# A graph network's two expert layers: branch arms for eight widths, and row fetches queued earlier

## The chip, the core and the metric

The kernel runs on one core of a Trainium2 chip, in one launch. The metric is device time in microseconds (us). The engines are TensorE (PE, matmuls), VectorE (DVE), ScalarE (ACT), GpSimd (POOL, which also issues indirect DMAs) and SyncE (SP, which issues DMAs). Each has its own instruction stream; "PEldq" in the profile is the sequencer that feeds PE with instructions.

## What is computed

Two layers over 1250 nodes of 1024 features, all in float32. Each layer adds a graph convolution and an attention mix to x, and then a mixture of experts (cut; names shortened):

```python
x = x + gcn(xn, edges) + mix0(xn)
x = x + experts0(layernorm(x))
x = x + sage(xn, edges) + mix1(xn)
x = x + experts1(layernorm(x))

# experts0: 8 experts, each takes its best at most 391 tokens
top_g, tok_idx = top_k(gates.T, cap)
xe = x[tok_idx]
h = silu(xe @ gate_w[e]) * (xe @ up_w[e])          # 1024 -> 512
out[tok_idx] += (h @ down_w[e]) * top_g            # 512 -> 1024

# experts1: 8 experts, every token goes to its best 2, no cap
hidden = silu(h1) * h2                             # 1024 -> 256 each
y = sum(prob * (hidden @ w3[e]))                   # 256 -> 1024
```

How many tokens an expert gets depends on the data. For these inputs the first layer's experts get 318, 358, 263, 231, 330, 366, 391 (its cap) and 237. In the second layer an expert's tokens are cut into units of at most 512; of 12 possible units ten are used, with 276, 384, 131, 394, 1, 384, 173, 17, 384 and 356 tokens.

## The kernel before

Tokens lie along a matmul's columns: for a block of 128 hidden features, a weight tile of 128x128 is loaded and the tokens of the expert (n columns) are streamed past it, over eight blocks k of the 1024 input features. Since n is known only at run time, `by_width` (L192) writes each piece of work once per possible width, as arms of a binary tree of `tc.If`, and every engine that has work in it branches to the arm whose width is the smallest that holds the count.

**First experts (L859 to L900).** For each of 8 experts, and each of four blocks i of hidden features, one piece computes gate and up (L868: 8 logical matmuls each), then the SiLU on ACT (L870) and the product on DVE (L871). It has four arms, 248, 296, 344 and 392 columns. Down is two pieces of four output blocks of four logical matmuls each (L888), with a transpose of each bank by DVE. The rows of the next expert are fetched by POOL (`rows_for`) and transposed by DVE (`columns`); its weights, 2 MB each for gate, up and down, are loaded by SP as their buffers come free.

**Second experts (L1358 to L1424).** `units_from(u, ...)` writes unit u and calls itself for the next. A unit loads the weights of unit u+1, computes gate and up for two blocks of hidden features (L1383; a piece is both, in four arms of 128, 256, 384 and 512 columns), lets DVE transpose the rows of unit u+1 (`turn`, L1372, with arms of its own), and computes down (L1401) per block of 128 tokens, where the tokens are the stationary operand and 512 output features are the columns. Each block's result goes through `ye` (six buffers; DVE L1406 and ACT L1404) and is added to the output by an indirect DMA of POOL (L1407, the scatter). `fetch(u)` (L1345) issues on POOL the indirect DMAs that bring the rows of unit u, 32 at a time by quarters (12 for 384 tokens), into `xq1`, which has two buffers. From unit 5 on a unit lies in a `tc.If` of its own (`when`, L1329).

The order of instructions on each engine is that of the program, as far as a scheduler doesn't move independent ones; POOL works through fetches and scatters strictly in that order, and so does DVE through h3T (L1387), the turn and ye. `tc.keep_in_program_order` pins the weight loads.

Of the kernel before, what the change touches and what calls it, by code (L numbers as in the profile page):

```python
# [10 lines left out]
F32 = mybir.dt.float32  # L11
# [11 lines left out]
P = 128  # L23
N = 1250
D = 1024
KB = D // P
# [13 lines left out]
H1 = 256  # L40
CAP = 391
SLOTS = 392
WIDTHS = [248, 296, 344, SLOTS]
B = 32
NI = 13
NG = 4
# [3 lines left out]
UC = 4  # L50
NU = 12
COLS = NU * UC
COUNTS = [P * (c + 1) for c in range(UC)]
LN_EPS = 1e-5
EXACT = 4096.0

# [47 lines left out]
def network(tc: tile.TileContext, a: dict, out: bass.AP, env: SimpleNamespace, exact: bool):  # L104
    nc = tc.nc
# [6 lines left out]
    turn = [0]  # L112
# [8 lines left out]
    def bank(name):  # L121
        return psum.tile([P, 512], F32, name=name, tag="bank")
# [69 lines left out]
    def by_width(n, widths, work):  # L192

        if len(widths) == 1:
            return work(widths[0])
        m = len(widths) // 2
        with tc.If(n <= widths[m - 1]) as cmp:  # L197
            by_width(n, widths[:m], work)
        with cmp.Else():
            by_width(n, widths[m:], work)  # L200
# [602 lines left out]
    with s_route:  # L803
        quarters = x1n_d.rearrange("n (j f) -> (n j) f", j=4)
        with tc.tile_pool(name="moe0", bufs=1) as mp:
            def first_columns():

                xeT = mp.tile([P, KB, ROWS], F32, name="xeT", bufs=2)
                room = [mp.tile([P, NI, B, KB], F32, name=n).rearrange("p i c b -> p (i c b)") for n in ("xq", "ye")]
                for g in range(NG):  # L810
                    n = min(P, SLOTS - g * P)
                    xe = room[g // 3][:, g % 3 * D:(g % 3 + 1) * D]
                    nc.gpsimd.indirect_dma_start(
                        out=xe, out_offset=None, in_=x1n_d,
                        in_offset=bass.IndirectOffsetOnAxis(ap=idx[:, g:g + 1], axis=0))
                    for b0 in (0, 4):
                        pt = bank("pte")
                        for b in range(4):
                            nc.tensor.transpose(pt[:, b * P:b * P + n], xe[:n, b0 + b::KB], ident[:n, :n])
                        evac(xeT[:, b0:b0 + 4, g * P:g * P + n], pt.rearrange("p (b q) -> p b q", b=4)[:, :, :n])  # L820
                return xeT

            def rows_for(e):
                xq = mp.tile([P, NI, B, KB], F32, name="xq")
                for i in range(NI):
                    g = e * NG + i // 4
                    nc.gpsimd.indirect_dma_start(
                        out=xq[:, i].rearrange("p c b -> p (c b)"), out_offset=None, in_=quarters,
                        in_offset=bass.IndirectOffsetOnAxis(ap=idx_q[:, i % 4, g:g + 1], axis=0))
                return xq  # L830

            def columns(xq):
                xeT = mp.tile([P, KB, ROWS], F32, name="xeT", bufs=2)
                for i0 in range(0, NI, 4):
                    i1 = min(i0 + 4, NI)
                    nc.vector.transpose(xeT.rearrange("p b (i r) -> p i b r", r=B)[:, i0:i1],
                                        xq[:, i0:i1].rearrange("p i c b -> p i b c"))
                return xeT

            def weights(e):  # L840
                wg, wu = (wpool.tile([P, KB, I0], F32, name=n, tag="w") for n in ("wg", "wu"))
                for w, name in ((wg, "gate"), (wu, "up")):
                    nc.sync.dma_start(w, a[f"L0_ffn_{name}_w"][e].rearrange("(p k) f -> p k f", k=KB))
                wd = mp.tile([P, I0 // P, D], F32, name="wd")

                load = (nc.sync if e else nc.scalar).dma_start(wd, a["L0_ffn_down_w"][e].rearrange("(k p) f -> p k f", p=P))
                if e == 0:
                    tc.keep_in_program_order(load)
                return wg, wu, wd

            xeT = first_columns()
            ws = weights(0)

            number = [nc.values_load(taken[0:1, e:e + 1], min_val=0, max_val=CAP) for e in range(E)]
            for e in range(E):
                wg, wu, wd = ws
                hT = mp.tile([P, I0 // P, SLOTS], F32, name="hT")
                if e + 1 < E:
                    xq = rows_for(e + 1)  # L859
                for i in range(I0 // P):  # L860
                    ic = slice(i * P, (i + 1) * P)
                    pg, pu = bank("pgate"), bank("pup")
                    sg = mp.tile([P, SLOTS], F32, name="sg", bufs=2)

                    def gate_up(n):
                        for pw, w in ((pg, wg), (pu, wu)):
                            for k in range(KB):
                                nc.tensor.matmul(pw[:, :n], w[:, k, ic], xeT[:, k, :n],  # L868
                                                 start=(k == 0), stop=(k == KB - 1))
                        nc.scalar.activation(sg[:, :n], pg[:, :n], AF.Silu)  # L870
                        nc.vector.tensor_mul(hT[:, i, :n], sg[:, :n], pu[:, :n])  # L871

                    by_width(number[e], WIDTHS, gate_up)
                    if i == 1:

                        wdb = mp.tile([P, I0 // P, KB, P], F32, name="wdb")
                        for j in range(I0 // P):
                            nc.scalar.copy(wdb[:, j], wd[:, j].rearrange("p (q b) -> p b q", b=KB))  # L878
                if e + 1 < E:
                    xeT = columns(xq)  # L880
                ye = mp.tile([P, NI, B, KB], F32, name="ye")
                for b0 in range(0, KB, 4):
                    pys = [bank("py") for _ in range(4)]

                    def down(n):
                        for b, py in enumerate(pys, b0):
                            for i in range(I0 // P):
                                nc.tensor.matmul(py[:, :n], wdb[:, i, b, :], hT[:, i, :n],  # L888
                                                 start=(i == 0), stop=(i == I0 // P - 1))
                            nc.vector.memset(py[:, n:ROWS], 0.0)  # L890
                            nc.vector.transpose(ye[:, :, :, b], py[:, :ROWS].rearrange("p (i r) -> p i r", r=B))

                    by_width(number[e], WIDTHS, down)
                for j in range(4):
                    (nc.sync if e == E - 1 and j % 2 else nc.scalar).dma_start(
                        env.y_d[e * ROWS:(e + 1) * ROWS, j * KB * B:(j + 1) * KB * B].rearrange("(i r) f -> r i f", r=B),
                        ye[j * B:(j + 1) * B].rearrange("p i c b -> p i (c b)"))
                if e + 1 < E:
                    ws = weights(e + 1)
# [400 lines left out]
    with tc.tile_pool(name="moe1", bufs=2) as ep:  # L1300
# [28 lines left out]
        def when(u, work):  # L1329

            if u < 5:
                return work()
            with tc.If(number[u] >= 1):
                work()
# [22 lines left out]

        def units_from(u, xeT, ws, coming):  # L1358
            later = u + 1 < NU
            if u + 2 < NU:  # L1360
                coming.append(fetch(u + 2))
            if later:
                xq = coming.pop(0)
                xeT2 = ep.tile([P, KB, UC * P], F32, name="xeT1")
# [7 lines left out]
                    nc.vector.transpose(xeT2.rearrange("p b (i r) -> p i b r", r=B)[:, i0:i1],  # L1372
                                        xq[:, i0:i1].rearrange("p i c b -> p i b c"))

            def unit():
                if later:
                    when(u + 1, lambda: load_unit(ws2, which[u + 1], queues[u + 1][0]))
                for i in range(H1 // P):
                    def gate_up(n):
                        p1, p2 = bank("p1"), bank("p2")  # L1380
                        for pw_, off in ((p1, 0), (p2, H1)):
                            for k in range(KB):
                                nc.tensor.matmul(pw_[:, :n], w12[:, k, off + i * P:off + (i + 1) * P], xeT[:, k, :n],  # L1383
                                                 start=(k == 0), stop=(k == KB - 1))
                        sg = ep.tile([P, UC * P], F32, name="sg1")
                        nc.scalar.activation(sg[:, :n], p1[:, :n], AF.Silu)
                        nc.vector.tensor_mul(hT[:, i, :n], sg[:, :n], p2[:, :n])  # L1387

                    by_width(number[u], COUNTS, gate_up)
                if later:  # L1390
                    when(u + 1, lambda: by_width(number[u + 1], COUNTS, turn))

                def down(n):
                    sent = []
                    for c in range(n // P):
# [21 lines left out]
                if later and u == NU - 2:  # L1417
                    units_from(u + 1, xeT2, ws2, coming)

            when(u, unit)  # L1420
            if later and not (u == NU - 2):
                units_from(u + 1, xeT2, ws2, coming)

        units_from(0, xeT, ws, [fetch(1)])  # L1424
    s_moe.close()


# [47 lines left out]
```

## Time and profile before

| | |
|---|---|
| median of 3 runs | 3427.32 us (3417.03 to 3428.79) |
| the profiled execution | 3425.42 us |
| its span, first to last instruction | 3423.7 us |
| mean granted TensorE clock | 0.968 |
| first experts' matmuls | 1215.8 to about 1655 us |
| second experts' matmuls | 3118.1 to 3402.9 us |
| bytes moved by DMA | 317.59 MB, 93 GB/s on average |

In a group's row, "x512" is the number of instructions, the three numbers are the shortest, median and longest in ns, and the shapes follow with their counts. A row of waits reads "engine, what waited <- what it waited for: total us, times, longest". A row of the timeline gives start, duration, engine, line and operation, and in brackets the idle time before it and what ended that. A wait "<- issue" is one for which the trace shows no semaphore: the engine's own sequencer had not delivered the instruction. Matmul durations overlap, since they are pipelined; the time from one start to the next is what one costs.

### The profile page before, as it was taken

Reading aid. Unit: us, or ns where it says so; the run is one execution under the profiler, and the core shown is the slowest. Engines: PE = TensorE matmul, PEld = TensorE weight load, DVE = VectorE, ACT = ScalarE, POOL = GpSimd, SP = SyncE. Lnnn points to the kernel's source line nnn. Section 1 sums busy time; section 2 is a strip of 40 time slices with the busy share of each in tenths; the row PEclk is TensorE's granted clock in tenths of the full one; section 3 lists DMA queues with packets and bytes.
Section 4 is the critical chain, followed back from the end, with each engine's and each line's share of the span. In section 5 each row is a group of like instructions: output and inputs, shape, how many; then the busy total and the mean of one; then the engine's idle time right before and its main releaser. Section 6 shows DMA issues by size and latency. Waiting matters only on the chain. (4 is left out here: it accounts for less than half of the span.)

```text
span 3423.7 us, 30825 instructions
## 1 busy us (share of the span) xinstructions
PE 3254.8 (95%) x11704; PEld 1966.0 (57%) x11704; DVE 941.5 (27%) x2398; ACT 359.2 (10%) x623; POOL 635.7 (19%) x543
## 2 busy tenths in 40 slices
PE   6999999999999789999699999999999999996987
PEld 3474656554557556766445555447777555564553
DVE  4148335531113632322440000011111111234221
ACT  1001011100004211111111011000000000001100
POOL 0006787032001041210100000110000000004432
PEclk9999999999998689999899999999999999997998
DMA  4715222054114054653640000220000110126662
GB/s 155 161 62 138 25 1 26 25 161 143 64 45 144 32 202 149 207 193 111 187 150 25 25 25 25 74 99 28 25 25 25 37 59 32 72 92 235 180 194 53
DMA packets 147591, 317.59 MB, mean 93 GB/s; under 512 B 38951, under 2 KB 60366, under 8 KB 143884
## 3 DMA queue, kind: packets, MB, share of 16 engines
q1 hardware_dynamic: 82108, 216.85, 18.6%
q0 software_dynamic: 40240, 48.25, 7.1%
q10 hardware_dynamic: 24992, 49.16, 4.7%
q8 instruction: 156, 2.56, 0.3%
q14 instruction: 95, 0.78, 0.1%
HBM read 239.25 MB, written 77.82 MB: 93 GB/s over the span
## 5 line engine op out<-in xcount | busy, mean ns | idle before, releaser
L276 POOL DMA_INDIRECT adj_d<-cnt,cell x167 | 261.4, 1565 | 89.3 <-issue 40.6
L1383 PE MATMUL p<-xeT,w 128*128 128x384 f32 (+3 forms) x640 | 179.0, 442 | 9.8 <-DVE ye L1406 5.9
L189 POOL TENSOR_TENSOR xr<-xr,bo 128x512 f32<-128x512 f32 (+1 forms) x40 | 50.4, 1265 | 712.4 <-DMA xr<-res_d 543.2
L1383 PEld LDWEIGHTS p<-xeT,w 128*128 128x128 f32 x640 | 114.0, 194 | 77.0 <-issue 27.0
L165 PE MATMUL pqk<-wk,x0T 128*128 128x512 f32 (+1 forms) x320 | 145.4, 609 | 8.9 <-ACT x0T L117 7.5
L868 PE MATMUL pgate<-xeT,wg 128*128 128x392 f32 (+3 forms) x512 | 151.0, 449 | 2.3 <-DVE py L890 2.0
L888 PE MATMUL py<-hT,wdb 128*128 128x392 f32 (+3 forms) x512 | 145.8, 444 | 4.1 <-ACT wdb L878 4.0
L868 PE MATMUL pup<-xeT,wu 128*128 128x392 f32 (+3 forms) x512 | 148.2, 443 | 0.0
L165 PE MATMUL pv<-wv,x1T 128*128 128x512 f32 (+1 forms) x320 | 141.9, 601 | 4.5 <-ACT x1T L117 2.5
L165 PE MATMUL ph<-ws,h1T 128*128 128x512 f32 (+1 forms) x320 | 143.2, 596 | 0.0
L165 PE MATMUL pqk<-wq,x0T 128*128 128x512 f32 (+1 forms) x320 | 140.7, 593 | 0.0
L165 PE MATMUL ppn<-wn,x1T 128*128 128x256 f32 (+1 forms) x640 | 138.8, 379 | 0.0
L1064 PE MATMUL ph<-x1T,ws 128*128 128x416 f32 (+1 forms) x384 | 138.2, 512 | 0.0
L165 PE MATMUL pv<-wv,x0T 128*128 128x512 f32 (+1 forms) x320 | 138.0, 592 | 0.0
L165 PE MATMUL ph<-wgcn,x0T 128*128 128x512 f32 (+1 forms) x320 | 138.0, 593 | 0.0
L165 PE MATMUL pwo<-wo,attn0T 128*128 128x512 f32 (+1 forms) x320 | 137.7, 593 | 0.2 <-ACT attn0T L433 0.2
L165 PE MATMUL ppn<-wn,h1T 128*128 128x512 f32 (+1 forms) x320 | 137.7, 592 | 0.0
L165 PE MATMUL pwo<-wo,attn1T 128*128 128x512 f32 (+1 forms) x320 | 137.5, 592 | 0.0
L940 PE MATMUL pqT<-x1T,wk 128*128 128x416 f32 (+1 forms) x384 | 135.6, 512 | 0.0
L940 PE MATMUL pqT<-x1T,wq 128*128 128x416 f32 (+1 forms) x384 | 135.6, 512 | 0.0
L165 PEld LDWEIGHTS ppn<-wn,x1T 128*128 128x128 f32 (+1 forms) x640 | 120.0, 188 | 17.7
L868 PEld LDWEIGHTS pgate<-xeT,wg 128*128 128x128 f32 x512 | 98.7, 193 | 49.4 <-issue 4.8
(383 smaller groups left out, 4469.3 us busy)
## 6 DMA issues: line engine op xcount, KB each, us to landing
wg<-in_L_ffn_gate_w_dram SPq DMA_DIRECT2D x8, 2048.0 KB
wu<-in_L_ffn_up_w_dram SPq DMA_DIRECT2D x8, 2048.0 KB
w<-in_L_ffn_w_dram SPq DMA_DIRECT2D x8, 2048.0 KB
wd<-in_L_ffn_down_w_dram SPq DMA_DIRECT2D x7, 2048.0 KB
y_d<-ye ACTq DMA_DIRECT2D x30, 416.0 KB
adj_d<-ezero SPq DMA_DIRECT2D x2, 6105.0 KB
res_d<-xr SPq DMA_DIRECT2D x45, 256.0 KB
table<-adj_d ACTq DMA_DIRECT2D x36, 312.5 KB
```

The lines of the kernel that those rows point to most:

```text
L165: nc.tensor.matmul(pr[:TS[t], :cols], xT[:, k, TOK[t]], w[:, k, :], start=(k == 0), stop=(k == nk - 1))
L189: nc.gpsimd.tensor_add(xr[:TS[t]], xr[:TS[t]], bias[:TS[t]])
L276: nc.gpsimd.indirect_dma_start(out=adj_d[e % 2], out_offset=bass.IndirectOffsetOnAxis(ap=cell[:, e:e + 1], axis=0), in_=cnt[:, e:e + 1], i ...
L868: nc.tensor.matmul(pw[:, :n], w[:, k, ic], xeT[:, k, :n], start=(k == 0), stop=(k == KB - 1))
L888: nc.tensor.matmul(py[:, :n], wdb[:, i, b, :], hT[:, i, :n], start=(i == 0), stop=(i == I0 // P - 1))
L940: nc.tensor.matmul(pq[:, :n], w[:, k, pair * P:(pair + 1) * P], xT[:, k, c0:c0 + n], start=(k == 0), stop=(k == KB - 1))
L1064: nc.tensor.matmul(ps[:, :n], w[:, k, q0 + f * P:q0 + (f + 1) * P], xT[:, k, c0:c0 + n], start=(k == 0), stop=(k == KB - 1))
L1383: nc.tensor.matmul(pw_[:, :n], w12[:, k, off + i * P:off + (i + 1) * P], xeT[:, k, :n], start=(k == 0), stop=(k == KB - 1))
```

## The change

First experts: the widths become eight, 224 to 392 in steps of 24. Gate and up become pieces of their own, and down becomes four pieces of two output blocks instead of two of four. Second experts: gate and up get eight widths from 64 to 512 in steps of 64 and are pieces of their own; where a width is not a whole block of 128, DVE zeroes the rest of the block in h3T, since down keeps whole blocks. The fetch for a unit is written two calls ahead instead of one: `fetch(u + 3)` stands between the turn of unit u+1 and the down of unit u, ahead of that unit's scatters, and `unit` is cut in two for it.

```diff
-WIDTHS = [248, 296, 344, SLOTS]
+WIDTHS = [224, 248, 272, 296, 320, 344, 368, 392]
...
+WIDTHS1 = [64, 128, 192, 256, 320, 384, 448, 512]
...
-                    def gate_up(n):
-                        for pw, w in ((pg, wg), (pu, wu)):
-                            for k in range(KB):
-                                nc.tensor.matmul(pw[:, :n], w[:, k, ic], xeT[:, k, :n],
-                                                 start=(k == 0), stop=(k == KB - 1))
+                    def product(p, w, n):
+                        for k in range(KB):
+                            nc.tensor.matmul(p[:, :n], w[:, k, ic], xeT[:, k, :n], start=(k == 0), stop=(k == KB - 1))
+
+                    def gate(n):
+                        product(pg, wg, n)
                         nc.scalar.activation(sg[:, :n], pg[:, :n], AF.Silu)
+
+                    def up(n):
+                        product(pu, wu, n)
                         nc.vector.tensor_mul(hT[:, i, :n], sg[:, :n], pu[:, :n])
 
-                    by_width(number[e], WIDTHS, gate_up)
+                    by_width(number[e], WIDTHS, gate)
+                    by_width(number[e], WIDTHS, up)
...
-                for b0 in range(0, KB, 4):
-                    pys = [bank("py") for _ in range(4)]
+                for b0 in range(0, KB, 2):
+                    pys = [bank("py") for _ in range(2)]
...
-            if u + 2 < NU:
-                coming.append(fetch(u + 2))
...
-            def unit():
+            def up_to_down():
                 if later:
                     when(u + 1, lambda: load_unit(ws2, which[u + 1], queues[u + 1][0]))
                 for i in range(H1 // P):
...
+                    def gate1(n):
+                        product(p1, 0, n)
                         nc.scalar.activation(sg[:, :n], p1[:, :n], AF.Silu)
+
+                    def up1(n):
+                        product(p2, H1, n)
+                        m = -(-n // P) * P
                         nc.vector.tensor_mul(hT[:, i, :n], sg[:, :n], p2[:, :n])
-
-                    by_width(number[u], COUNTS, gate_up)
-                if later:
-                    when(u + 1, lambda: by_width(number[u + 1], COUNTS, turn))
-
+                        if n < m:
+                            nc.vector.memset(hT[:, i, n:m], 0.0)
+
+                    by_width(number[u], WIDTHS1, gate1)
+                    by_width(number[u], WIDTHS1, up1)
+
+            when(u, up_to_down)
+            if later:
+                when(u + 1, lambda: by_width(number[u + 1], COUNTS, turn))
+
+            if u + 3 < NU:
+                coming.append(fetch(u + 3))
+
+            def from_down():
                 def down(n):
...
-            when(u, unit)
+            when(u, from_down)
...
-        units_from(0, xeT, ws, [fetch(1)])
+        units_from(0, xeT, ws, [fetch(1), fetch(2)])
```

More of the change, by code (lines that the diff above doesn't have):

```diff
@@ L1378, in unit, with product @@
                 for i in range(H1 // P):
[L1379 to L1385, printed above, removed]
+                    p1, p2 = bank("p1"), bank("p2")
+                    sg = ep.tile([P, UC * P], F32, name="sg1")
+                    def product(p, off, n):
+                        for k in range(KB):
+                            nc.tensor.matmul(p[:, :n], w12[:, k, off + i * P:off + (i + 1) * P], xeT[:, k, :n],
+                                             start=(k == 0), stop=(k == KB - 1))
+                    def gate1(n):
+                        product(p1, 0, n)
                         nc.scalar.activation(sg[:, :n], p1[:, :n], AF.Silu)
+                    def up1(n):
+                        product(p2, H1, n)
+                        m = -(-n // P) * P
                         nc.vector.tensor_mul(hT[:, i, :n], sg[:, :n], p2[:, :n])
-                    by_width(number[u], COUNTS, gate_up)
-                if later:
-                    when(u + 1, lambda: by_width(number[u + 1], COUNTS, turn))
+                        if n < m:
[8 more added lines that the diff above has]
+            def from_down():
                 def down(n):
```

## The prediction

> **What bounds the kernel now.** I read the page's first two parts, then the groups by line, then the waits of TensorE (PE) in the two stages that the diff touches, then the branch records of its sequencer and the timeline where it stood still.
>
> ```profile
> PE 3254.8 (95%) x11704; PEld 1966.0 (57%) x11704; DVE 941.5 (27%) x2398; ACT 359.2 (10%) x623; POOL 635.7 (19%) x543
> ...
> q8 instruction: 156, 2.56, 0.3%
> ```
>
> PE is busy 95% of 3423.7 us, so matmul time that is taken away is time gained, unless PE then waits for something. Queue 8 brings code: 156 fetches of 2.56 MB in all, 16,384 bytes each. It looks harmless as a share; I come back to it.
>
> ```profile
> L868 PE MATMUL pgate<-xeT,wg x512: 372/453/913, 1215.8 to 1636.4; 128*128 128x392 f32 x64, 128*128 128x344 f32 x43, 128*128 128x248 f32 x43, 128*128 128x296 f32 x21
> L1383 PE MATMUL p<-xeT,w x640: 273/486/1008, 3118.1 to 3392.0; 128*128 128x384 f32 x80, 128*128 128x256 f32 x32, 128*128 128x128 f32 x32, 128*128 128x512 f32 x16
> ```
>
> These durations are of overlapping, pipelined matmuls. From start to start one takes 209 ns at 248 columns, 249 at 296, 289 at 344, 329 at 392, 323 at 384 and 429 at 512: 0.84 ns per column. Each logical f32 matmul is two recorded ones: 192 per first expert (64 gate, 64 up, 64 down), 64 gate and up per second unit and 8 per block of 128 rows in its down. In the first stage PE waits only 6 us in all. In the second (3118 to 3424):
>
> ```profile
> PE py L1401 <- DVE h3T L1387: 6.3, 1, 6.3
> PE p L1383 <- DVE ye L1406: 5.9, 2, 5.3
> PE p L1383 <- issue: 3.9, 1, 3.9
> PE py L1401 <- issue: 0.8, 1, 0.8
> ```
>
> The first is unit 7 at 3328.7: DVE stood 5.40 us in the turn (L1372) for unit 8's rows, and this unit's h3T was queued behind it. The second is unit 0 at 3149.4: DVE stood 5.88 us for unit 1's rows, with ye (L1406) behind it. The "issue" ones are PE's own sequencer:
>
> ```profile
> L197 PEldq COMPARE_BRANCH  x265: 64/179/5449, 1215.3 to 3395.0; - x133
> ```
>
> ```profile
> 3251.52 7.31 PE L1383 MATMUL p<-xeT,w 128*128 128x128 f32 x64
> ...
> 3258.66 3.60 PE L1401 MATMUL py<-w,h3T 128*128 128x512 f32 x8
> ...
> 3266.12 1.62 PE L1383 MATMUL p<-xeT,w 128*128 128x384 f32 x2 [3.86 <-issue]
> ```
>
> A branch usually takes 64 to 450 ns, but some took 3.92, 4.80, 5.14 and 5.45 us. The last began at 3260.38, after unit 4, whose matmuls are only 128 wide: PE ran dry for 3.86 us. Beside the fetch records the reason shows. Code comes one block ahead: the fetch of the next block starts when the sequencer enters a block, and a branch into it ends about 1.4 us after its transfer of 1.0 us is over. From entering to start is 1.05 us in most of the first stage, but 3.6 to 3.9 us while the next expert's weights load (1320 to 1330: DMA share 1.0, 400 GB/s), and in the second stage between 3180 and 3335 a median of 4.1 us. A block per 3.5 us is thus the pace in quiet stretches, 6.2 to 6.5 us in busy ones. What covers it is the lead: the sequencer runs 18 recorded matmuls ahead of the array, 5.2 us at 344 columns, 7.7 us behind 512-wide downs, 2.0 us at 128.
>
> **The change, part by part.** The sum is against the profiled execution's 3425.4 us; the median of the runs shown is 3427.3, 1.9 us above it.
>
> *Widths in the first experts.* The counts in the inputs are 318, 358, 263, 231, 330, 366, 391 and 237; the widths go from 344, 392, 296, 248, 344, 392, 392, 248 to 320, 368, 272, 248, 344, 368, 392, 248. Four experts lose 24 columns: 4 x 192 x 24 x 0.84 ns = **-15.5 us**, all on PE's path, since PE hardly waits there.
>
> *Widths in the second units.* Counts 276, 384, 131, 394, 1, 384, 173, 17, 384, 356. Gate and up lose 64 columns in units 0, 2, 3 and 6: 64 x 64 x 0.84 ns = 3.4 us each. Unit 0's is lost again: its end waits for rows whose fetch PE doesn't release, and that wait grows by what PE saves. So **-10.3 us**. Units 4 and 7 go from 128 to 64 columns; what says what that is worth? A 128-wide f32 matmul here starts each 112 ns, and so do the 65-wide ones at L368 and even 8-wide ones: no gain. [...] The row decides: 0. Down keeps whole blocks of 128.
>
> *Row fetches ahead of scatters.* In the built order only two things move on POOL: unit 8's 12 fetches go ahead of the scatters of units 4 and 5, unit 9's ahead of those of 5 and 6. On DVE both h3T now precede the turn. So unit 7's wait goes: **-6.3 us**. The scatters they pass (units 4 to 6, 6 instructions) come later by 12 fetches x 1.25 us = 15 us; ye has 6 buffers, and the scatters of the last units stay last, so nobody waits: 0. Loads on SP are not moved. The memsets of the tails (two per partial unit, some 0.1 us each) sit before down: **+0.5 us**. In the first stage DVE's three turns come 4 operations earlier and down's fourths have two banks; DVE is far from full (27%): 0.
>
> *The code.* A piece of by_width was one arm in four of 32 matmuls; it is now one in eight of 16. All arms of a piece lie one behind the other, so a piece spans about the same code as before, one block (48 pieces in the first stage, 50 fetches), and is passed in half the time. Counted in the built programs, PE passes 103 blocks in the first stage instead of 49, and 49 instead of 27 in the second. [...]
>
> First stage. A piece of 16 takes 3.34 us at 248 columns, 3.66 at 272, 4.3 at 320, 4.6 at 344, 4.9 at 368, 5.3 at 392. In quiet stretches it needs 1.06 x 3.5 = 3.7 us: only 248 is short, by 0.36. During the 16 us in which the next weights (6 MB) load it needs 1.06 x 6.2 = 6.6 us, for 2.4 pieces: short by 2.4 x (6.6 - piece) = 7.8, 7.1, 5.5, 4.8, 4.0 and 3.2 us. The lead (3.8, 4.1, 4.8, 5.2, 5.6, 5.9 us) covers the wide ones, which win it back in their quiet pieces; 272 and 248 don't. That leaves 0.7 (first expert), 3 (third), 7.8 + 9.6 x 0.36 = 11.3 (fourth, no lead left) and 0.5 (eighth) = 15.5 us. The first expert also meets the saturated loads up to 1265; I take **+20**, between 1 (quiet pace throughout) and 35 (the busy stretch half as long again).
>
> Second stage. A unit needs 4 x 1.06 for gate and up and 0.7 for down (28 fetches in all before, less 21 for 20 pieces, over ten downs): 4.9 blocks. Units 0, 1, 3, 5, 8 and 9 have 27 to 38 us of matmuls and keep up, or hide behind unit 0's row wait. Units 2 and 6 have 64 x 0.161 + 16 x 0.429 = 17.2 us, units 4 and 7 64 x 0.112 + 8 x 0.429 = 10.6 us, in stretches with a DMA share near 0.8. At 6 us a block (a little under the measured 6.5, since a slower PE spreads the same transfers) 4.9 blocks take 29.4 us: short by 12.2, 18.8, 12.2 and 18.8 = 62 us; a lead of 7.7 us covers part in units 2, 4 and 6 (unit 7 follows a unit that has used it): 39 us. The 4.6 us of issue waits of today are in it: **+34**. Ends: +2 at the quiet pace (only unit 7 is 6.6 short), +45 at 6.5.
>
> Sum: -15.5 - 10.3 - 6.3 + 0.5 + 20 + 34 = +22.4, **3448 us**.
>
> **The rivals.**
> - *The code stays hidden: faster.* The place is the same branches. The quiet pace of 3.5 us holds, since slower-running units leave gaps in the DMA. Then the cost is 1 + 2 us, and 3425.4 - 31.6 + 3 = about 3397; with a few busy blocks 3405. For it: in the first stage today none of the long branches cost anything, and queue 8's share is 0.3%. Against it: even with half the crossings, second units run dry. It decides if the pace in units 4 to 7 stays under 4 us a block. Chance 0.2.
> - *Saturated pace everywhere.* 35 + 45 - 31.6 + 0.5 = +49: 3474, and more if single fetches start 8 us late, as one did at 3260. Chance 0.2.
> - *The row wait isn't removed, or comes back.* PE's stops shift the fetches and a later turn waits for rows instead: +6.3 on the forecast, 3454. For it: fetches wait for a buffer that the turn frees. Against: 15 us are gained for each. Chance 0.1.
>
> The forecast itself has 0.5, with 3425 to 3465.
>
> **How the numbers follow.** 0.5% (17 us) is about what a measurement of this kernel can tell from no change. Faster by more (below 3410) is the first rival's most: 0.19. Within it (3410 to 3444) is the lower part of the forecast and the rest of the first rival: 0.26. Slower: 0.55. The range 3403 to 3486 leaves out about 1 in 10 on either side; where the sign is open, the likeliest case's own range is 3425 to 3465.
>
> **What would show it.** Queue 8 rises from 156 fetches to some 230 or more. PE's busy time falls by about 29 us (15.5 + 13.8), in rows of 320, 368 and 272 columns. PE's waits "issue" in the second stage grow from 4.7 to some 40 us, most at units 4 and 7; in the first stage some 20 us, in the third and fourth expert. The wait for h3T of 6.3 us is gone, and the fetches of unit 8 start before the scatter of unit 4. I am wrong if branch records stay under 3 us, if issue waits lie elsewhere than in narrow pieces, or if PE waits for DVE or ACT.

## The result and the profile after

The changed kernel takes 3460.84 us (median of four runs, 3459.71 to 3462.04), against 3423.22 for the kernel before on the same chip: 1.011 times as long, 95% interval 1.0089 to 1.0132. The profiled execution took 3462.04 us, its span 3460.3; that is 36.6 us more than the profiled one of before.

The page's first part and the code queue, after:

```profile
PE 3252.6 (94%) x11704; PEld 1972.8 (57%) x11704; DVE 941.8 (27%) x2410; ACT 358.1 (10%) x623; POOL 634.3 (18%) x543
...
q8 instruction: 234, 3.83, 0.5%
```

PE works through the same 11704 matmuls, many of them narrower, and yet its busy time has fallen by 2 us only, where the columns alone were to take off 29. Code fetches went from 156 to 234, as forecast. PE's waits, in the first experts (1216 to 1675) and then the second (3141 to 3439):

```profile
PE py L894 <- issue: 16.2, 9, 3.3
PE pgate L868 <- issue: 3.4, 2, 1.7
PE pup L868 <- issue: 3.1, 3, 1.4
```

```profile
PE p L1388 <- issue: 13.0, 7, 3.9
PE py L1421 <- issue: 9.0, 3, 4.1
PE p L1388 <- DVE ye L1426: 5.9, 1, 5.9
PE p L1388 <- DVE h3T L1400: 1.5, 1, 1.5
PE py L1421 <- DVE h3T L1398: 1.3, 1, 1.3
```

Waits for "issue" are 22.7 us in the first stage, where there were none, and 22.0 in the second, where there were 4.7. The 6.3 us behind unit 8's rows are gone; the 5.9 us at the end of unit 0 stay. The sequencer's branches and the timeline of unit 4 (tokens: 1) say why:

```profile
L198 PEldq COMPARE_BRANCH  x613: 64/187/6204, 1215.6 to 3430.7; - x154
```

```profile
3277.59 5.49 PE L1388 MATMUL p<-xeT,w 128*128 128x64 f32 x48
...
3286.94 3.67 PE L1388 MATMUL p<-xeT,w 128*128 128x64 f32 x16 [3.86 <-issue]
...
3294.72 6.35 PE L1421 MATMUL py<-w,h3T 128*128 128x512 f32 x8 [4.12 <-issue]
```

Three of the four gate and up pieces run through on the lead; then PE stands until the fourth piece's code is there, and again until down's. In the first stage it is the same in the down pieces of the fourth expert (248 columns), each ahead of 16 matmuls:

```profile
1424.46 3.58 PE L894 MATMUL py<-hT,wdb 128*128 128x248 f32 x16 [2.89 <-DVE xeT L837]
1430.69 3.61 PE L894 MATMUL py<-hT,wdb 128*128 128x248 f32 x16 [2.64 <-issue]
1437.59 9.74 PE L894 MATMUL py<-hT,wdb 128*128 128x248 f32 x32 [3.29 <-issue]
```

The first of these waits carries DVE's name, but DVE's transpose of the next rows runs beside it; the sequencer was in branches of 5.69, 5.21 and 6.20 us there, and each time the matmuls start within 0.6 us of that branch's end.

There is a second loss, which the sum did not have. After some of the waits PE starts at half pace. Starts (us) of PE's matmuls after the wait that ends at 1385.5 (third expert, 272 columns):

```
1385.512  1386.119  1386.572  1387.025  1387.479  1387.932  1388.385  1388.749  1388.979
```

They are 453 ns apart and then, from 1388.7 on, 229. The windows of the trace (stretch, length, busy times, then clock, DMA share, GB/s) show the granted clock of that stretch, and of one before it:

```profile
1385.50:1388.70 3.20, 3.19 (x7) 2.50 (x8) 0.00 (x0) 0.00 (x0) 2.39 (x3) 0.51 0.44 122
1379.00:1382.50 3.50, 3.50 (x16) 2.91 (x16) 2.88 (x5) 0.00 (x0) 2.59 (x3) 1.00 0.95 403
```

A matmul at half pace counts as busy, so this part doesn't appear as a wait. In the two stages of this profile all five waits of 3 us or more are followed by half the clock, and four of the seven between 2 and 3 us (2.04, 2.38, 2.55 and 2.62 us), which begins up to 1.4 us after the wait's end.

With the usual distance from start to start known for each width, every stage can be divided: what a start is late by counts as a wait where the distance is above 2.2 times the usual, and as slow matmuls below that. In us, from the first to the last start:

| stage | before | after | columns (forecast of the diff) | waits | slow matmuls |
|---|---|---|---|---|---|
| first experts | 439.4 | 458.5 | -15.5 | 7.5 -> 34.0 | 3.3 -> 11.3 |
| second experts | 284.2 | 297.0 | -13.8 | 19.2 -> 34.4 | 6.9 -> 18.3 |

-15.5 + 26.5 + 8.0 = +19.0 (measured 19.1), and -13.8 + 15.2 + 11.4 = +12.8 (measured 12.8). Of the 19.4 us more in slow matmuls, 15.2 lie where the trace grants half the clock; the rest are matmuls late by less. The columns were saved to the last microsecond: 320, 368, 272 and 344 columns now start every 269, 309, 229 and 289 ns. The remaining 4.7 of 36.6 us lie outside the two stages: 3.2 between them (1463.0 before, 1466.2 after) where the diff changes nothing. The kernels below, equal there, show between 1464.3 and 1468.3 on chips of like speed, so this is taken as scatter.

### The profile page after: what moved, and what is told of

It is laid out like the page before. It is cut to its first block, busy times and chain, and to the rows that moved or that the text cites. A ratio compares the mean times of both kernels' runs of the same rounds, so it can differ in the third digit from the quotient of the medians.

```text
span 3460.3 us, 32647 instructions
## 1 busy us (share of the span) xinstructions
PE 3252.6 (94%) x11704; PEld 1972.8 (57%) x11704; DVE 941.8 (27%) x2410; ACT 358.1 (10%) x623; POOL 634.3 (18%) x543
## 5 line engine op out<-in xcount | busy, mean ns | idle before, releaser
L1388 PE MATMUL p<-xeT,w 128*128 128x384 f32 (+4 forms) x640 | 172.9, 434 | 20.6 <-issue 13.0
L894 PE MATMUL py<-hT,wdb 128*128 128x368 f32 (+5 forms) x512 | 149.6, 450 | 22.0 <-issue 16.2
L868 PE MATMUL pgate<-xeT,wg 128*128 128x368 f32 (+5 forms) x512 | 146.1, 439 | 5.1 <-issue 3.4
L868 PE MATMUL pup<-xeT,wu 128*128 128x368 f32 (+5 forms) x512 | 143.5, 433 | 3.1 <-issue 3.1
L894 PEld LDWEIGHTS py<-hT,wdb 128*128 128x128 f32 x512 | 99.6, 198 | 70.8 <-issue 27.4
```

The lines of the kernel that those rows point to most:

```text
L868: nc.tensor.matmul(p[:, :n], w[:, k, ic], xeT[:, k, :n], start=(k == 0), stop=(k == KB - 1))
L894: nc.tensor.matmul(py[:, :n], wdb[:, i, b, :], hT[:, i, :n], start=(i == 0), stop=(i == I0 // P - 1))
L1388: nc.tensor.matmul(p[:, :n], w12[:, k, off + i * P:off + (i + 1) * P], xeT[:, k, :n], start=(k == 0), stop=(k == KB - 1))
```

## The experiments

Stage times below are taken as in the table. The theory ("code"): PE waits for blocks of code that come one at a time, so what counts is how much code its path passes per microsecond of matmuls. Rivals: twice as many branches and pieces cost by themselves; narrow matmuls do; dead code is free and the cost is elsewhere.

**The changed kernel with four old widths (e1).**

```diff
-WIDTHS = [224, 248, 272, 296, 320, 344, 368, 392]
+WIDTHS = [248, 296, 344, SLOTS]
-WIDTHS1 = [64, 128, 192, 256, 320, 384, 448, 512]
+WIDTHS1 = [128, 256, 384, 512]
```

> As after, but with the four old widths: twice as many pieces as before, each half as long in code and in matmuls (51 blocks of code in the first stage, 28 in the second, by the built program; before 50 and 27). Code theory (the loss is PE waiting for blocks of code): the first stage takes before's 439 us within 3, PE's issue waits there stay under 3 us; only the row wait of 6.3 us goes, so some 3415 us. Branch theory (the loss is the price of twice as many branches, pieces and semaphores): the first stage takes 450 us or more, total 3440 or more.

Measured: 3421.59 us, 0.9989 times before (0.998 to 0.9997). First stage 436.8 us, second 281.4, 160 fetches. Splitting the pieces and doubling the branches cost nothing; the first stage is 2.6 us shorter. The branch theory falls. Less was gained in the second stage than expected (2.8 of 8 us): unit 7 lost its wait for rows and went from 20.8 to 16.5 us, but 4.0 us of waits for issue and 2.6 for ye remain in it, and unit 4 is 3.0 us longer, with a wait of 4.0 us put down to DVE's turn.

**Eight arms on the old columns (e2).**

```diff
+    def old(works, steps):
+        return lambda n: works(min(s for s in steps if s >= n))
...
-                    by_width(number[e], WIDTHS, gate)
+                    by_width(number[e], WIDTHS, old(gate, [248, 296, 344, SLOTS]))
```

and so for up, down and the second stage's gate and up.

> As after in pieces, arms and code (103 and 50 blocks), but each of the eight arms works on the old number of columns, so no matmul is narrower than before. Code theory: the waits come without the saving, somewhat smaller since the pieces are longer: first stage 439 + 20 to 30 us, second stage 284 + 10 to 20, total 3450 to 3470. Width theory (narrow matmuls themselves are what PE can't sustain): close to before, 3410 to 3425.

Measured: 3475.53 us, 1.0143 (1.0124 to 1.0162). First stage 471.4 us, second 302.2, 234 fetches: the total and the first stage are a little above the upper ends, the second stage just inside. With no matmul narrower than before, the loss is all there: +32 us in the first stage (waits 33.7, slow matmuls 9.2). Wider pieces do not absorb more: experts four and five lost 13.1 and 7.9 us against before.

**The row fetches alone (e3).** Before's widths and pieces; the unit cut in two and `fetch(u + 3)` ahead of its scatters, as in the change.

> Before's widths and pieces, with only the unit cut in two and the row fetches queued ahead of the scatters. If the stall of unit 7 on the rows of unit 8 is all that moves: -6.3 us of the wait and -2 us of matmuls at half pace after it, 3415 us. If another row wait takes its place: within 3 us of before.

Measured: 3419.35 us, 0.9988 (0.998 to 0.9996). The second stage falls by 10.1 us, to 274.1: unit 7 from 20.8 to 14.9 us, 5.9 of the 8.3 forecast (the wait went, the half pace stayed), and units 0 and 1 by 5.3 together. Only 4 to 5 us reach the total: the matmuls of the second stage start 3.5 us later in this profile.

**The first experts' weights loaded once (e4).**

```diff
-                if e + 1 < E:
-                    ws = weights(e + 1)
```

> As after, but the first experts 1 to 7 don't load their own weights: all use those of expert 0, so 42 MB of transfers are missing in the first stage while PE's code and matmuls are the same. Contention theory (a block of code costs 6 us instead of 3.5 while weights load): the first stage falls from 458.5 to 432 to 440 us, and issue waits of more than 2.5 us in the down pieces are gone there. Fixed price (a block costs the same whatever else moves): it stays within 3 us of 458. The second stage stays as in after either way.

Measured: first stage 433.6 us, inside the forecast; waits 16.1 instead of 34.0, slow matmuls 4.3 instead of 11.3. PE's waits for issue ahead of down, with the loads (16.2 us in nine) and now without:

```profile
PE py L894 <- issue: 0.4, 1, 0.4
```

PE runs the same number of instructions of each kind there, so the price of a block depends on what else the DMA engines carry: contention is shown for the down pieces. What is left are experts three, four and eight (48.1, 48.6 and 45.2 us against 44.0, 40.1 and 39.9 of matmuls). In the third and fourth PE still waits 2.0 and 3.9 us for issue ahead of gate and up; whether that is the price of a block without contention, or the transfers that remain (rows in, results out), isn't separated. The total, 3423.14 us, isn't compared: with other values the second layer's experts get other tokens (it ran nine units).

**Eight arms with whole pieces (e5).** After's widths, but gate and up in one piece, down in halves.

> After's eight arms and its fetch order, but gate and up in one piece and down in halves, as before: half as many branches as after, and a piece of about two blocks of code; PE's path enters 88 blocks in the first stage instead of after's 103 and before's 50, 15 of them in both stages by a jump over a block. Code theory: nearly after's loss: first stage 447 to 458 us (after 458.5), second 285 to 297. Branch theory (the number of branches and pieces decides): the first stage saves its 15.5 us, 424 to 430.

Measured: 3514.96 us on a chip where the kernel before took 3459.05: 1.0174 (1.0157 to 1.0191), more than the change. First stage 479.5 us, second 308.5. Fewer branches didn't help. Both forecasts are missed, the code theory's by 21 us. PE's waits for issue in the first stage are 31.7 us (22.7 in the changed kernel), and 45 branches there take over 3 us where the changed kernel has 19: that fits pieces of two blocks, where more of the branches jump. Part of the excess may be this chip, see e7.

**One branch for an expert (e6).**

```diff
-                    by_width(number[e], WIDTHS, gate)
-                    by_width(number[e], WIDTHS, up)
...
-                    by_width(number[e], WIDTHS, down)
...
+                def expert(n):
+                    for i in range(I0 // P):
+                        (gate, up, SiLU, product; wdb; columns; down)
+                by_width(number[e], WIDTHS, expert)
```

and in the second stage one arm for a unit's gate and up.

> After's widths and fetch order, but one branch for a whole first expert (gate, up and down in one arm) and one for a second unit's gate and up. Static code is as long as after's, but PE's path enters 31 blocks in the first stage instead of 103 and 32 in the second instead of 50. Code theory: the widths' saving at last arrives: first stage 424 to 432 us, second 262 to 275, total 3395 to 3405. If it is the length of the static code or the widths that cost: 3440 or more.

Measured: 3531.68 us on the same chip, 1.0218 (1.0201 to 1.0235); first stage 481.9 us, second 320.8. Counting the blocks entered is not enough: there are 31 where after has 103, and the loss is larger. Branch records (start, us) at the fifth expert's end: 1500.88 3.41, 1504.77 4.67, 1509.50 5.88, three in a row; PE's timeline there:

```profile
1497.68 8.55 PE L883 MATMUL py<-hT,wdb 128*128 128x344 f32 x29
1515.68 0.95 PE L871 MATMUL pgate<-xeT,wg 128*128 128x368 f32 x1 [9.45 <-issue]
```

An arm is now one and a half blocks long, so the nodes of the tree lie far apart: the way out and the steps down to the arm are branches over whole blocks, and they take 3.2 to 6.5 us each, one after the other. The lead, 18 matmuls, covers about one. Ahead of the seventh expert there are four in a row (3.74, 4.03, 5.95 and 5.78 us). PE's wait of 14.9 us there carries the name of DVE's transpose, but at all six changes of expert with such branches PE's first matmul starts within 0.3 us of the last one's end. From the seventh expert, whose arm is the last of its tree, to the eighth, whose arm lies in the first quarter, no branch is long, and the eighth takes 40.0 us, its matmuls and nothing else. So code passed per microsecond accounts for the loss only while it is passed in order; here a jump over blocks cost 3.2 to 6.5 us by itself.

**Four arms at chosen widths, whole pieces (e7).** Before's pieces, after's fetch order.

```diff
+WIDTHS = [264, 336, 368, 392]
+WIDTHS1 = [128, 192, 384, 512]
```

> The fetch order of after and the pieces of before with four arms, but at widths chosen for these counts: 264, 336, 368, 392 in the first stage, 128, 192, 384, 512 in the second (units 2 and 6 at 192). Code as long as before's (50 and 27 blocks). Code theory: the saving comes whole: first stage 64 columns x 192 x 0.84 ns = 10.3 us less, 429; second stage 6.9 us less than the 274 of the run with the fetch order alone, less some 3 for units that are now short of code; total 3402 to 3410.

Measured: 3449.70 us, 0.9971 (0.9964 to 0.9979) of before on that chip. First stage 444.1 us, second 281.1, some 15 and 11 us above the forecast. Between the stages e5, e6 and e7 show 1483.5 to 1489.8 us where the other chips show 1463 to 1468: this chip is slower in parts that no kernel here changes, and there is no profile of before on it. In e7's first stage no branch takes over 2.9 us and PE waits 4.1 us for issue, so most of its 15 us is not a wait for code. How much of e5's excess belongs to the chip is open; e5's and e6's explanations rest on their branch records.

**Two arms fewer, four more (e8, e9).** The changed kernel without, or with more of, arms that no count takes:

```diff
+WIDTHS = [248, 272, 320, 344, 368, 392]                                            # e8
+WIDTHS1 = [64, 192, 320, 384, 448, 512]
...
+WIDTHS = [200, 208, 216, 224, 248, 272, 296, 320, 344, 368, 376, 392]              # e9
+WIDTHS1 = [64, 80, 96, 112, 128, 192, 224, 256, 320, 384, 448, 512]
```

> After without the arms that these counts never take (224 and 296 in the first stage, 128 and 256 in the second): the same matmuls, pieces and branches taken, but 77 and 39 blocks of code on PE's path instead of 103 and 50. Code theory (a block per 3.5 us in quiet stretches, 6 in busy ones, less the lead): first stage 428 to 436 us, second 270 to 284, total 3405 to 3425 on a chip where after takes 3461. If dead code is free, it is after's time.

> After with four more arms in each stage that no count takes: same matmuls, 154 and 65 blocks. Code theory: the first stage becomes bound by code nearly throughout, 154 x 3.5 = 539 us and up to 590 with the busy stretches; second stage 350 to 390; total 3620 to 3690. If dead code is free, it is after's time; if only another level of compares costs (0.2 us each), within 10 us of it.

Measured, with the changed kernel run again beside them (e10):

> The changed kernel once more, on the same chip as the runs beside it, so that they can be compared directly: 1.011 times before, whatever the theory.

| kernel | time, us | times before | first stage | second stage | code fetches |
|---|---|---|---|---|---|
| e8, six arms | 3424.89 | 1.0003 (0.9995 to 1.0011) | 426.9 | 294.2 | 197 |
| e10, after | 3465.08 | 1.011 (1.009 to 1.013) | 458.0 | 300.5 | 234 |
| e9, twelve arms | 3652.05 | 1.0663 (1.0641 to 1.0684) | 602.4 | 336.5 | 308 |

The matmuls that run are the same in all three; only code that never runs differs. Four dead arms a piece cost 187 us, and two fewer save 40. The first stage at six arms is 1 us below its forecast; at twelve it is 12 us above the upper end and needs 602 us for 154 blocks, 3.9 us each, between the quiet and the busy pace. Its waits for issue, over the whole stage (1218.3 to 1821.6 us):

```profile
PE py L894 <- issue: 59.8, 18, 6.7
PE pgate L868 <- issue: 26.0, 9, 4.3
PE pup L868 <- issue: 21.0, 10, 3.3
```

That dead code is free, and that the compares as such cost, is refuted. The second stage doesn't follow the count so well: from six to eight arms it moves by 3 to 6 us where 13 or more were expected, and at twelve it is 14 us below its forecast. Units 4 and 7 take 21.7 and 23.2 us at six arms, as many as at eight (23.6 and 20.5 in the profile after), and unit 0's wait for rows is 10.7 us instead of 5.9. With six arms the branches in these two units still take 5.67, 4.56, 4.45 and 4.95 us, and the clock granted in them is 0.76 and 0.63. Why two arms fewer bring nothing there is open.

**Four chosen arms with split pieces (e11).** As e7, with after's pieces.

> Four arms at widths chosen for these counts (264, 336, 368, 392; 128, 192, 384, 512) with after's smaller pieces and fetch order: 51 and 28 blocks. Code theory: faster than before by 10.3 us of columns in the first stage, 6.9 in the second, 6 to 10 for the rows, less a few us in units 4, 6 and 7 which are short of code: 0.992 to 0.996 times before. Branch theory: no faster than 1.000.

Measured: 3406.08 us, 0.9941 (0.9922 to 0.996), the fastest of all, 18 us under before. First stage 426.2 us with waits of 5.2, second 275.6, 160 fetches. Less code per piece and fewer columns can be had together, as long as four arms do: these four are chosen for these counts.

## Why the prediction was right, and where it was off

The direction and the mechanism held: slower, by PE waiting for code at narrow pieces, with the columns' saving real and the row wait gone. The forecast of +22 us against the profiled execution became +36.6, 4.7 of it outside the two stages. By its own terms:

- *Columns, first experts, -15.5:* right (matmuls of the four experts start 20 ns closer). *Second units, -10.3, unit 0's share lost to its row wait:* right; unit 0 takes 38.0 us instead of 36.5 with 3.4 us less to do. *No gain at 64 columns:* right, a 64-wide matmul starts each 112 ns as the 128-wide one did. What sets this floor isn't shown; a weight load's record is 190 ns long (L868).
- *Row fetches, -6.3:* right, and e3 shows 10 us in the stage by itself, 4 to 5 in the total.
- *Code, first stage, +20 (1 to 35):* the term that was mis-sized; it measured 26.5 of waits and 8.0 of slow matmuls, 34.5 in all. The step was "leaves 0.7 (first expert), 3 (third), 11.3 (fourth) and 0.5 (eighth)". Against their columns the third lost 10.0 us and the fourth 12.3, the eighth 3.4, and the first and the four wide ones 8.8 together. The third, forecast at 3, is the largest miss. Its gate and up pieces of 3.66 us were taken as level with a quiet pace of 3.5 us a block. Undisturbed and one after the other, fetches come even faster, 3.1 us apart (starts at 1357.48, 1360.61 and 1363.65). But the stretch before was not quiet: with other transfers under way they start 5.0 and 5.1 us apart (1347.35, 1352.34 and 1357.48). Busy times, clock, DMA share and GB/s of the two stretches:

```profile
1347.40:1357.40 10.00, 9.49 (x43) 7.71 (x42) 0.44 (x1) 0.40 (x1) 0.00 (x0) 1.00 0.63 129
1357.50:1363.70 6.20, 4.48 (x21) 3.42 (x20) 0.44 (x1) 0.00 (x0) 0.00 (x0) 1.00 0.02 6
```

PE stood for 0.51 us at 1355.1 and, behind a branch of 4.23 us, for 1.72 us at 1360.2. The lead was gone, and the down pieces met the weight loads without it.

- *Code, second stage, +34:* it measured 18.6 us of waits other than for rows (7.2 before, 25.8 after, unit 0 left out, since it ends with its rows), and 11.4 of slow matmuls: 30 in all. Near, but by luck, since two errors offset each other: the waits were put too high, and half pace was not in the sum at all. The waits for issue at units 2, 4 and 6 (3.9, 8.0 and 3.8 us) are not far from what the lead was to leave (4.5, 11.1 and 4.5); at unit 7, which was to have no lead, they are 3.9 instead of 18.8. In both stages slow matmuls are 19.4 us, over half of the change.
- Two slips that don't move the forecast: the rival "saturated pace everywhere" adds the +0.5 of the memsets twice, and the stretch 1320 to 1330 has a DMA share of 0.94 and 387 GB/s, not 1.0 and 400.

The clock had been in the page of before (at unit 7, after the 6.3 us wait, six matmuls at half pace, 2.4 us), and I read only the wait. In the trace after, the granted clock is 0.50 from 1385.24 to 1388.65, 3.41 us, behind a wait of 2.62 us; behind the wait of 2.29 us before that it stayed at 1.00, and so it did behind waits of 2.64 and 2.89 us in the next expert, while one of 2.04 us in the first was followed by the half. The length of the wait alone doesn't tell which below 3 us.

What the kernel before showed after unit 4, a branch of 5.45 us in which a code transfer began only after 3.05 us, and PE idle for 3.86, was the right thing to weigh against this change, and e6 is its plainest case: three long branches in a row, and PE idle for 9.45 us. Of the rivals, the one in which the code stays hidden is refuted by the 44.7 us of waits for issue and by e8 and e9; saturation everywhere is nearest for the third and fourth expert, and e4 shows that it is saturation in their down pieces. The wait of 6.3 us for unit 8's rows did not come back.

## What to carry to other kernels

An arm that never runs cost here what its code takes to be passed (187 us for four a piece, e9): before adding arms to a branch on PE, multiply the blocks of code in a piece by the time that a block takes (3 to 6 us here), and compare that with the piece's matmul time at the narrowest width. Fewer, better placed widths beat many (e11), and if pieces are merged, the branch's own nodes must stay close together (e6). Count a wait of PE of 3 us or more together with the slow matmuls that follow it (five of five here).

## What the runs showed of the hardware

- Where code is the bound (e9, first stage), the fetches of two blocks of code (16,384 bytes each) start at least 3.0 us apart, in the median 3.4 and on average 3.9, although a transfer takes 1.0 us (median, before and after).
- Beside other transfers fetches come further apart: without the weight loads the waits for issue ahead of the first stage's down pieces fall from 16.2 to 0.4 us. In the changed kernel fetches start 5.0 us apart at a DMA share of 0.63 and 3.1 us apart at 0.02.
- In the changed kernel's first stage each of the 33 branches of over 2.5 us ends 1.3 to 1.5 us after the end of a code transfer. In e6 branches over blocks take 3.0 to 6.5 us, and 7.7 once; several in a row add up (3.41, 4.67 and 5.88 us, ahead of 9.45 us in which PE is idle).
- After waits of 3 us or more (five of five in the changed kernel's two stages), and of some of 2 to 3 (four of seven), PE's matmuls run at half the clock for 3.41 us or a multiple of it (3.41, 6.83 and 13.65 us in that trace). Of 17 and 32 slow matmuls in the two stages before, 9 and 17 fall in such stretches, of 70 and 110 after 35 and 83, and of 230 and 196 with twelve arms 177 and 158.
